# Two chunks of rows gathered ahead of a branch: a two-layer graph convolution on one core

## The chip, the cores and the metric

One core of a Trainium2 chip runs the whole program in one launch. The metric is device time in microseconds of one execution; lower is better. The engines are PE (matrix products and transposes), PEld (PE's weight loads), DVE (vector), ACT (scalar functions), POOL (which here issues the gathers) and SP (which only issues transfers). Each engine works through its own instructions in the order in which the program emits them, and waits where an input or a buffer isn't ready.

## The reference

The graph has 6250 nodes with 128 features and 106250 edges, sorted by their target `dst`. Each edge has 64 attributes and a weight. Two transformer convolutions with 2 heads of 64 follow each other, with a batch normalisation and a ReLU between them; the result is added to x and normalised by rows:

```python
rel_t = last_update[src] - t                       # last_update is node_vec, t is edge_weight
edge_attr = concatenate([cos(rel_t[:, None] * time_w + time_b), msg], -1)    # 32 + 64 columns
# _transformer_conv(h, ...):
q, k, v = h @ Wq + bq, h @ Wk + bk, h @ Wv + bv    # in 2 heads
e = edge_attr @ We
alpha = einsum('ehc,ehc->eh', q[dst], k[src] + e) / sqrt(C)
a = softmax of alpha over the edges of one dst
out = segment_sum((v[src] + e) * a, dst) + h @ Ws + bs
# whole:
h = relu(batch_norm(conv1(x)));   return layernorm(x + conv2(h))
```

So an edge needs the row of features of its source node and, in the first convolution, that node's time.

## The kernel before, in words

**Preparation.** `tile_gnn_resnorm` loads the edge lists (`srows`, `drows`, `erows`: 104 rows of 1024 edges), x and the first convolution's weights. The loads are issued by SP and ACT; every transfer that these two issue uses one of eight semaphores in turn, so an issue waits until the one eight transfers earlier has landed. `columns` turns an edge list so that an edge stands on its partition: `srcs`, `dsts`, `ew`. `load_features` brings x into SBUF in four blocks (`cuts`), in the room that later holds h (`fhT`), with a free column ahead of each row; `pass_features` copies the nodes' times into that column, block by block, and stores rows of 129 numbers to DRAM as `xv_d`. In between, DVE works out the chunks' first nodes (`nbs`) and checks that the edge list has the shape that the fast path needs (`edge`, `worst`, `oki`). Then come `matrices` (products of the weights), `codes`, and `tables` for the first 512 nodes (`tab_d`, `skip_d`).

**The branch.** If the check holds, `ordered` runs; otherwise `general`, which isn't run here.

**`ordered`.** First `turn_features` turns x by 128x128 transposes on PE into `xT`, four to a bank, copied out by DVE and ACT in turn. Then `conv(0)` and `conv(1)` go over 104 chunks of 1024 edges (8 tiles of 128). Per chunk: `fetch` has SP load the attributes, the table and more into the chunk's buffers (`s.f`: the edge's terms `s.e` and its rows `s.x`); `gather` has POOL issue 8 indirect transfers, one for each 128 edges, which bring the source rows from `xv_d` (in `conv(0)`) or from h (in `conv(1)`); `encode` works out the cosine's angles on DVE from the times in column 0 of the rows, and `sine` finishes them on ACT; `turn_rows` and `turn_terms` transpose rows and terms on PE; `score`, `lowest`, `weigh`, `turn_weights`, `gather_sums`, `divide`, `finish_turn` and `product` make the softmax and the sums.

**The order.** It is written out by hand: in round k PE scores chunk k, sums chunk k-1 and turns the rows of chunk k+1, DVE makes the angles of chunk k+2 (later k+3), and POOL gathers chunk k+4 (AHEAD, `lead`). In `conv(0)` rounds -4 to -1 fill the pipeline. From round -1 on the gathers of a chunk are tied one by one to PE's steps of the round (`bring` with `behind`), so that they keep PE's pace. `pull(extra, n)` slips in the work of `rest()`: `targets` (which of a chunk's sums goes to which node) and `tables` for the further blocks of nodes, one product per pull, two pulls in rounds 0 to 3 and one later.

The buffers `ff` come from a pool of 7 in `conv(0)` and of 6 in `conv(1)`.

## Time and profile before

| | |
|---|---|
| median of 3 runs | 2173.48 us (2171.8 to 2174.38) |
| profiled execution, its own time | 2172.61 us |
| its span in the profile | 2170.8 us |
| mean granted clock of PE | 0.878 |
| busy: PE, PEld, DVE, ACT, POOL | 76%, 45%, 51%, 45%, 73% |
| first and last gather of `conv(0)` | 32.77 us, 1070.43 us |
| first gather of `conv(1)` | 1104.59 us |

How to read the rows: in the order of time a row gives start and length in us, engine, line of the kernel, operation, output<-inputs, the number of instructions, and in brackets the idle time ahead and what ended it. SPq and ACTq are the issues of transfers on SP and ACT. In a row of waits stand the sum in us, how often, and the longest. In a row by line stand the count, the shortest, median and longest in ns, and the first and last start in us. In a table of stretches stand each engine's busy us with its count, the granted clock of PE, the share of the transfer engines and GB/s. Releasers are inferred, and where the one named had long been done it was another.

### The profile page before, as it was taken

Reading aid. Unit: us, or ns where it says so; the run is one execution under the profiler, and the core shown is the slowest. Engines: PE = TensorE matmul, PEld = TensorE weight load, DVE = VectorE, ACT = ScalarE, POOL = GpSimd, SP = SyncE. Lnnn points to the kernel's source line nnn. Section 1 sums busy time; section 2 is a strip of 40 time slices with the busy share of each in tenths; the row PEclk is TensorE's granted clock in tenths of the full one; section 3 lists DMA queues with packets and bytes.
Section 4 is the critical chain, followed back from the end, with each engine's and each line's share of the span. In section 5 each row is a group of like instructions: output and inputs, shape, how many; then the busy total and the mean of one; then the engine's idle time right before and its main releaser. Section 6 shows DMA issues by size and latency. Waiting matters only on the chain.

```text
span 2170.8 us, 46552 instructions
## 1 busy us (share of the span) xinstructions
PE 1644.0 (76%) x13253; PEld 975.1 (45%) x13253; DVE 1109.6 (51%) x3706; ACT 970.0 (45%) x1830; POOL 1577.5 (73%) x1684
## 2 busy tenths in 40 slices
PE   4877787867877778787768778777777877777776
PEld 3545454544545445554535434443344434433333
DVE  4866667656666666776747333333333333332233
ACT  1766666655555545566643333333332333232322
POOL 3777777777777777777547777777777777777774
PEclk9899999889999998999988888888888888888888
DMA  7777777777777777777758667676677667667663
GB/s 208 196 223 215 208 227 210 209 198 208 197 208 198 221 214 214 199 216 212 213 161 239 186 180 188 184 198 178 185 192 191 184 188 191 180 189 191 171 162 79
DMA packets 426852, 423.89 MB, mean 195 GB/s; under 512 B 297304, under 2 KB 344258, under 8 KB 423258
## 3 DMA queue, kind: packets, MB, share of 16 engines
q1 hardware_dynamic: 352622, 272.49, 44.0%
q0 software_dynamic: 53184, 109.45, 21.4%
q10 hardware_dynamic: 20780, 38.87, 5.0%
q8 instruction: 109, 1.79, 0.3%
q14 instruction: 157, 1.29, 0.2%
HBM read 274.73 MB, written 142.54 MB: 192 GB/s over the span
## 4 chain that ended last, share of the span: by engine, by line
PE 35%; DMA 35%; DVE 14%; issue 8%; POOL 5%; ACT 2%; SPq 0%; DVEq 0%; ACTq 0%; POOLq 0%
DMA ff<-hn_d,fsrcs 20%; DMA ff<-xv_d,fsrcs 10%; PE fpa L1017 10%; PE fps L970 8%; POOL ff L855 5%; PE fpx L927 5%; PE fpg L632 4%; DVE farg L899 3%; PE fpe L939 2%; PE fpa L1048 2%; DVE fa L1029 1%; PE fppt L994 1%; DVE fangles L897 1%; DVE fangles L896 1%; DVE farg L894 1%
## 5 line engine op out<-in xcount | busy, mean ns | idle before, releaser
L855 POOL DMA_INDIRECT ff<-xv_d,fsrcs x831 | 785.6, 945 | 282.4 <-issue 113.1
L855 POOL DMA_INDIRECT ff<-hn_d,fsrcs x775 | 733.5, 947 | 236.3 <-issue 99.7
L927 PE MATMUL fpx<-fident,ff 128*128 128x128 f32 x1664 | 330.3, 310 | 234.2 <-DMA ff<-hn_d,fsrcs 223.3
L1017 PE MATMUL fpa<-ff,fpt 128*32 128x256 f32 (+1 forms) x4128 | 406.4, 447 | 0.0
L931 ACT COPY fft<-fpx 128x512 f32<-128x512 f32 x402 | 233.2, 580 | 360.0 <-PE fpx L927 357.1
L927 PEld LDWEIGHTS fpx<-fident,ff 128*128 128x128 f32 x1664 | 227.1, 155 | 295.3 <-DMA ff<-hn_d,fsrcs 247.2
L995 ACT COPY fpt<-fppt 128x384 f32<-128x384 f32 x208 | 99.8, 480 | 486.0 <-PE fppt L994 435.6
L970 PE MATMUL fps<-fft,ftab 128*32 128x384 f32 (+1 forms) x1774 | 262.0, 521 | 47.2 <-ACT fs L985 40.5
L1017 PEld LDWEIGHTS fpa<-ff,fpt 128*32 128x32 f32 (+1 forms) x4128 | 141.0, 127 | 263.7 <-issue 186.7
L1048 PE MATMUL fpa<-fsel,fa 128*128 128x128 f32 x404 | 87.9, 302 | 172.8 <-DVE fsel L1033 172.7
L1098 DVE TENSOR_SCALAR fout<-fres,fmean,fvar 64x128 f32<-64x128 f32 x104 | 36.8, 355 | 348.4 <-ACT fvar L1096 342.2
L978 DVE TENSOR_REDUCE flow<-fps 128x1 f32<-128x384 f32 x207 | 114.8, 555 | 83.6 <-PE fps L970 81.9
L939 PE MATMUL fpe<-fident,ff 128*112 128x128 f32 x832 | 145.4, 305 | 2.1 <-ACT ff L906 2.1
L940 ACT COPY fet<-fpe 112x512 f32<-112x512 f32 x207 | 123.1, 595 | 50.4 <-DMA et_d<-fet 34.5
L892 DVE TENSOR_TENSOR frel<-ff,few 128x8 f32<-128x8 f32 x104 | 18.1, 174 | 245.6 <-DMA ff<-xv_d,fsrcs 245.0
L970 PE MATMUL fps<-fet,ftab 112*32 112x384 f32 (+2 forms) x960 | 141.9, 459 | 0.0
L899 DVE SCALAR_TENSOR_TENSOR farg<-fangles,farg 128x256 f32<-128x256 f32 x312 | 132.3, 424 | 10.7
L1048 PEld LDWEIGHTS fpa<-fsel,fa 128*128 128x128 f32 x404 | 48.5, 148 | 193.4 <-DVE fsel L1033 193.3
L970 PEld LDWEIGHTS fps<-fft,ftab 128*32 128x32 f32 x1774 | 85.2, 118 | 108.4 <-ACT fs L985 52.7
L994 PE MATMUL fppt<-fident,fs 128*128 128x128 f32 x626 | 111.5, 288 | 18.2 <-DVE fbits L845 11.2
L985 ACT ACTIVATE fs<-fps,fm 128x384 f32<-128x384 f32 x207 | 120.4, 582 | 6.9 <-DVE fm L980 5.9
L970 PE MATMUL fps<-fxT,ftab 112*32 112x384 f32 (+2 forms) x900 | 119.0, 500 | 0.3 <-DMA fxT<-et_d 0.3
(264 smaller groups left out, 2446.1 us busy)
## 6 DMA issues: line engine op xcount, KB each, us to landing
ea_d<-ff SPq DMA_DIRECT2D x104, 448.0 KB
et_d<-fet SPq DMA_DIRECT2D x104, 448.0 KB
ff<-ea_d SPq DMA_DIRECT2D x104, 448.0 KB
fxT<-et_d SPq DMA_DIRECT2D x104, 448.0 KB
tab_d<-fo ACTq DMA_DIRECT2D x26, 1024.0 KB
ftab<-tab_d SPq DMA_DIRECT2D x832, 32.0 KB
ff<-in_edge_attr SPq DMA_DIRECT2D x103, 256.0 KB
ff<-xv_d,fsrcs POOLq DMA_INDIRECT x831
```

The lines of the kernel that those rows point to most:

```text
L855: row = nc.gpsimd.indirect_dma_start(out=f[:, t, :D + 1 - c], out_offset=None, in_=(h_d[:N, :] if k < RAW else hn_d) if c else pl.xv_d, in ...
L899: nc.vector.scalar_tensor_tensor(arg, turn, -part, arg, op0=OP.mult, op1=OP.add)
L927: last = nc.tensor.transpose(px[:, t * P:(t + 1) * P], s.x[:, u * 4 + t, 1 - c:1 - c + D], ident)
L931: nc.scalar.copy(s.ft[:, u * GE:(u + 1) * GE], px)
L939: last = nc.tensor.transpose(pe[:EC, t * P:(t + 1) * P], s.e[:, u * 4 + t], ident)
L940: copy(s.et[:, u * GE:(u + 1) * GE], pe[:EC])
L970: steps.append(nc.tensor.matmul(s.ps[r, to:to + n], s.tab[:kd, r, i], (ets if i else fts)[:kd, at:at + n], start=i == 0, stop=i == 1 and t ...
L978: nc.vector.tensor_reduce(low, s.ps, AX.X, OP.min)
L985: nc.scalar.activation(s.s[:, :s.ps.shape[1]], s.ps, AF.Exp, bias=s.bias, scale=-1.0)
L994: last = nc.tensor.transpose(pp[:, t * P:(t + 1) * P], s.s[:, t * P:(t + 1) * P], ident)
L1017: steps.append(nc.tensor.matmul(s.pa[g * GH:(g + of) * GH].rearrange("p (a d) -> p a d", a=2), s.pt[:, (g * n + t) * GH:(g * n + t + of) * ...
L1048: step = nc.tensor.transpose(s.po[:, i], s.a[:, r], s.sel[:, 0])
```

## The change

1. **Rows of two chunks ahead of the branch** (EARLY = 2). As soon as `srcs` is there, POOL issues 16 gathers from x itself, into columns 1 to 128 of the first two chunks' rows. The buffers are no longer pool tiles: `got.ring` holds 7 slots (RING) for both convolutions and is made with the program's lasting buffers; `split_rows` hands out a slot. `gather` returns at once for these two chunks, and in `conv(0)` chunks below 7 are no longer tied to PE's steps.
2. **Their times by 0/1 products.** `pick_times` brings the nodes' times as a 49x128 table (`hours`, two more loads on SP). For each 512 edges a product of a 0/1 row with the upper part of the source's number spreads it over 49 partitions, DVE compares it with the lane, four products with `hours` pick the row of 128 times, and four DVE instructions weigh it with the comparison of the lower part and sum it into column 0. They use two banks of their own (`ftm`).
3. **x is turned in the preparation.** `turn_features` becomes a generator with one bank (`fxp`); ACT alone copies. It, `pick_times`, `codes`, `matrices` and `pass_features` are advanced step by step, in an order written out between the steps of the check.
4. **Loads.** `tail` goes behind the weights on ACT; the first 512 rows of x (`x0`) and the edge weights (`erows`) go from ACT to SP, behind x and ahead of the stores to `xv_d`.
5. `matrices` gets twelve pieces of three banks instead of two banks in turn. `targets` takes two pulls instead of one. `columns(drows)` and `columns(erows)` come later. In `conv(1)` there are 7 buffers `ff` instead of 6, `fout` has 4 instead of 6, and `fhn` alternates with `fhr`. `general` takes its room from the ring.

The core of the diff:

```diff
+RING = 7
+EARLY = 2
 def turn_features(nc, pl, bank, N):
-    nc.vector.memset(xT[:, N:], 0.0)
     for b0 in range(0, NF, 4):
-        px = mp.tile([P, 4, P], F32, name="fpx")
+        px = bank().rearrange("p (i n) -> p i n", n=P)
         for i in range(n):
             nc.tensor.transpose(px[:, i], pl.rows[:, b0 + i, 1:], pl.ident)
-        eng = nc.scalar.copy if b0 // 4 % 2 else nc.vector.tensor_copy
-        eng(lanes[:, b0:b0 + n], px[:, :n])
+        nc.scalar.copy(lanes[:, b0:b0 + n], px[:, :n])
+        yield
+def pick_times(nc, pl, pool, bank, srows, node_vec):
+    hi_i = pool.tile([EARLY, CE], I32, name="fhi")
+    nc.vector.tensor_scalar(hi_i, srows[:EARLY], 7, None, op0=OP.arith_shift_right)
...
+    yield
+    for k in range(EARLY):
+        times = split_rows(pl, k)[2]
+        for u in range(T // 4):
+            pb = bank()
+            nc.tensor.matmul(pb[:NA], one[:, k], hi[:, u * GE:(u + 1) * GE], start=True, stop=True)
+            oh = pool.tile([NA, GE], F32, name="foh", bufs=2)
+            nc.vector.tensor_scalar(oh, pb[:NA], lane[:NA], None, op0=OP.is_equal)
+            yield
+            pc = bank().rearrange("p (i n) -> p i n", n=P)
+            for i in range(4):
+                nc.tensor.matmul(pc[:, i], oh[:, i * P:(i + 1) * P], pl.hours, start=True, stop=True)
+            for i in range(4):
+                nc.vector.scalar_tensor_tensor(junk, pl.place_of, lo[:, t, k:k + 1], pc[:, i], op0=OP.is_equal,
+                                               op1=OP.mult, accum_out=times[:, t, 0:1])
+            yield
-            s.f = load.tile([P, T * FW], F32, name="ff")
+            s.f, s.e, s.x = split_rows(pl, k + c * NC)
         def gather(k, rows, behind=None):
             f = ch[k].x
+            if c == 0 and k < EARLY:
+                return
-                        gather(j, rows, behind)
+                        gather(j, rows, behind if c or j >= RING else None)
-        with tc.tile_pool(name="ftp", bufs=3, space=bass.MemoryType.PSUM) as mp, tc.manual_schedule():
-            turn_features(nc, pl, mp, N)
         columns(srows, srcs)
+        for k in range(EARLY):
+            to = split_rows(got, k)[2]
+            for t in range(T):
+                nc.gpsimd.indirect_dma_start(out=to[:, t, 1:], out_offset=None, in_=x,
+                                             in_offset=bass.IndirectOffsetOnAxis(ap=srcs[:, t, k:k + 1], axis=0))
         passed = pass_features(nc, got, made, N)
+        step(hours)
+        step(code)
         picked = pl.tile([NC, 2 * NQ], F32, name="picked")
...
+        step(passed)
+        step(code)
+        step(turned, 2)
         starts = pl.tile([1, NC + 1, NQ], F32, name="starts")
...
+        step(hours)
+        step(passed)
+        step(turned)
+        step(mats, 2)
         edge = pl.tile([1, 11], F32, name="edge")
...
+        step(passed)
+        step(hours)
+        step(turned, 2)
+        step(hours)
         ends = pl.tile([1, 2, NQ], F32, name="ends")
...
+        step(mats)
+        for _ in passed:
+            pass
+        step(turned)
         down = pl.tile([NC, CE], F32, name="down")
...
+        step(mats, 2)
+        pb = small[0][0:1, 0:1]
...
+        for _ in mats:
             pass
         xT0 = pl.tile([P, GE], F32, name="fxT0")
...
+        step(turned)
+        columns(drows, dsts)
+        table = tables(nc, got, 0, xT0, 0, mw, wide)
+        step(table, 4)
+        step(turned)
+        step(hours)
+        columns(erows, ew)
+        step(table)
+        step(hours)
+        step(turned)
+        for _ in hours:
+            step(turned)
+        for _ in turned:
+            pass
```

More of the change, by code (lines that the diff above doesn't have):

```diff
@@ L72, in general @@
 def general(ctx: ExitStack, tc: tile.TileContext, x, src, dst, edge_attr_64, edge_weight, node_vec,
-            time_w, time_b, conv1, conv2, bn_g, bn_b, out):
+            time_w, time_b, conv1, conv2, bn_g, bn_b, out, room, columns):
     nc = tc.nc
@@ L131, in general @@
     nc.sync.dma_start(ew, edge_weight.rearrange("(p j) -> p j", j=EC))
-    xall = const.tile([P, NB, D], F32, name="xall")
+    xall, skip = (room[:, i * NB * D:(i + 1) * NB * D].rearrange("p (b d) -> p b d", d=D) for i in range(2))
     if NR:
@@ L168, in general @@
     step = RW * GT * (-(-64 // GT))
-    zeros = op.tile([P, step], F32, name="zeros")
+    zeros = columns[:, :step]
     nc.gpsimd.memset(zeros, 0.0)
@@ L687, in ordered @@
     et_d = dram.tile([NC, EC, CE], F32, name="et_d")
-    xT = pl.xT = const.tile([P, NP], F32, name="fxT")
+    xT = pl.xT
     def bounds(j):
@@ L877, in hide @@
             for b0 in hidden[:n]:
-                step = put_rows(hn_d, b0, *turned_rows(b0, small.tile([P, GE // P, P], F32, name="fhn", bufs=4)))
+                rows = small.tile([P, GE // P, P], F32, name="fhn", bufs=2) if b0 % 2 else None
+                step = put_rows(hn_d, b0, *turned_rows(b0, rows))
             del hidden[:n]
@@ L1350, in rest @@
             others = second()
-            targets()
+            yield from targets()
             yield
@@ L1493, in tile_gnn_resnorm @@
                                                              ap=[[1, 1], [QE, NQ - i]]))
[L1494 to L1497 removed]
+        x0 = pl.tile([P, GE // P, D], F32, name="fx0")
+        nc.sync.dma_start(x0, x[:GE, :].rearrange("(b p) d -> p b d", p=P))
+        rows(nc.sync, erows, edge_weight, CE)
         got.wv = [keep.tile([P, D], F32, name=f"fwv{c}") for c in (0, 1)]
@@ L1538, in columns, with step @@
                 nc.vector.tensor_copy(to[:, t0:t0 + 4], pt)
+        def step(gen, n=1):
+            for _ in range(n):
+                next(gen, None)
         columns(srows, srcs)
-        passed = pass_features(nc, got, made, N)
+        for k in range(EARLY):
[3 more added lines that the diff above has]
+                                             in_offset=bass.IndirectOffsetOnAxis(ap=srcs[:, t, k:k + 1], axis=0))
+        passed = pass_features(nc, got, made, N)
+        hours = pick_times(nc, got, pl, aside, srows, node_vec)
+        code = codes(nc, got, keep, mw, bank)
+        turned = turn_features(nc, got, turning, N)
+        mats = matrices(nc, got, 0, keep, bank, pl)
+        step(hours)
+        step(code)
         picked = pl.tile([NC, 2 * NQ], F32, name="picked")
@@ L1611, in tile_gnn_resnorm @@
         nc.vector.tensor_scalar(oki, tot, 0.0, None, op0=OP.is_equal)
-        columns(drows, dsts)
-        for _ in matrices(nc, got, 0, keep, bank, pl):
+        for _ in mats:
             pass
-        codes(nc, got, keep, mw, bank)
         pt = wide()
@@ L1621, in tile_gnn_resnorm @@
         nc.vector.tensor_copy(xT0, pt)
-        for _ in tables(nc, got, 0, xT0, 0, mw, wide):
+        step(turned)
[11 more added lines that the diff above has]
+        for _ in turned:
             pass
-        columns(erows, ew)
         got.tw = broadcast(nc, keep, "ftw", time_w, TD)
```

76 lines of the change are left out of this document (50 added, 26 removed).

## The prediction

> **What bounds the kernel now.** I read the row gathers by their line, then what POOL waited for, the order of time at the start and in the first rounds, and the chain of waits there. The profiled execution took 2172.61 us, its span 2170.8; the median of the runs, 2173.48, lies 0.9 above. The sum is made against 2172.61, then carried over. For this kernel 0.2% (4.3 us) is about what a measurement can tell from no change.
>
> ```profile
> L855 POOL DMA_INDIRECT ff<-xv_d,fsrcs x831: 940/944/1121, 32.8 to 1070.4; - x167
> ```
>
> ```profile
> L855 POOL DMA_INDIRECT ff<-hn_d,fsrcs x775: 940/944/1421, 1177.9 to 2146.4; - x194
> ```
>
> ```profile
> POOL ff L855 <- issue: 99.7, 327, 0.3
> ...
> POOL ff L855 <- DMA ff<-xv_d,fsrcs: 18.3, 60, 0.3
> ```
>
> The last fence is what POOL waited for from 100 to 1050 us, the longest wait last: 0.3 us, never more than the gap between two issues. 831 gathers from 32.8 to 1070.4 are one each 1.25 us, and the 775 of convolution 1 that read hn_d keep the same pace. Convolution 0 is a POOL stream: what starts it earlier, or takes gathers from it, ends it earlier, as long as nobody else stands in its way. Convolution 1 follows that end and keeps its length.
>
> **The start, in order of time.**
>
> ```profile
> 8.96 1.28 DVE L1538 CAST fsrcs<-fpx 128x416 int32<-128x416 f32 x2 [1.05 <-PE fpx L1537]
> ...
> 18.68 0.57 DVE L1575 SCALAR_TENSOR_TENSOR most<-prior,nbf 1x412 f32<-1x412 f32 x1
> 19.18 0.07 DVE L1575 DVE_READ_ACCUMULATOR most<-prior,nbf 1x1 f32 x1
> ...
> 20.00 0.34 ACTq L556 DMA_DIRECT2D fbs<-in_L_gnn_bs  x1
> ...
> 20.38 0.59 ACTq L1606 DMA_DIRECT2D fx<-in_x  x1
> ...
> 20.81 3.47 SPq L533 DMA_DIRECT2D xv_d<-fhT  x3
> ...
> 22.62 1.22 DVE L1598 TENSOR_REDUCE worst<-down 104x1 f32<-104x1024 f32 x1
> 23.42 1.02 ACTq L1484 DMA_DIRECT2D erows<-in_edge_weight  x1
> ...
> 24.47 1.28 ACT L588 ACT_TABLE_LOAD   x1 [24.47 <-DMA xv_d<-fxrest]
> 24.55 0.14 DVE L1611 TENSOR_SCALAR oki<-tot 1x1 int32<-1x1 f32 x1
> ...
> 26.68 0.23 PEld L585 LDWEIGHTS fpt<-fident,fwq 128*128 128x128 f32 x1
> ...
> 30.48 0.50 PEld L600 LDWEIGHTS fpt<-ftr,ftr 64*128 64x128 f32 x2 [0.34 <-DVE fb L606]
> ...
> 32.77 1.11 POOL L855 DMA_INDIRECT ff<-xv_d,fsrcs  x1 [29.35 <-DMA fwv<-in_L_gnn_Wv]
> ...
> 35.56 4.46 PE L632 MATMUL fpx<-fxT,fm 128*128 128x512 f32 x6 [0.78 <-DVE fxT L1621]
> ...
> 42.72 0.38 ACTq L644 DMA_DIRECT2D tab_d<-fo  x1
> ...
> 43.96 0.57 PE L1537 MATMUL fpx<-fident,erows 104*128 104x104 f32 x4 [0.69 <-DVE few L1538]
> ...
> 44.58 0.59 DVE L1538 COPY few<-fpx 128x416 f32<-128x416 f32 x1 [0.67 <-PE fpx L1537]
> 45.37 2.31 PEld L658 LDWEIGHTS fpx<-fident,fhT 128*128 128x128 f32 x12 [1.03 <-issue]
> ...
> 48.52 1.02 ACT L660 COPY fxT<-fpx 128x512 f32<-128x512 f32 x1 [4.63 <-DMA ftab<-tab_d]
> ```
>
> POOL has the source columns at 10.2 us but waits until 32.77 for the rows with times (xv_d), whose last store is issued by 24.28. ACT issues loads until 24.44. The flag for the branch stands at 24.69, DVE ends the preparation at 45.17, and only then x is turned, on DVE and ACT.
>
> **The change, part by part.**
>
> *Sixteen gathers leave the stream.* 16 x 1.25 = 20.0 us, done in POOL's idle time from about 10 to 30 us. Their cover is the wait to 32.77; were it gone they would cost those 20 us again.
>
> *Gate 1, the store of xv_d.* It still holds chunk 2. Two things make it later. Transfers:
>
> ```profile
> 0.00:10.00 10.00, 1.65 (x8) 1.33 (x8) 2.42 (x6) 0.00 (x0) 2.74 (x22) 1.00 0.85 194
> 10.00:20.00 10.00, 2.93 (x16) 1.85 (x16) 4.74 (x28) 0.00 (x0) 0.00 (x0) 1.00 1.07 283
> 20.00:30.00 10.00, 4.41 (x21) 3.65 (x21) 6.76 (x30) 2.04 (x4) 0.00 (x0) 1.00 0.92 342
> 30.00:40.00 10.00, 8.02 (x22) 4.39 (x20) 1.86 (x9) 2.87 (x5) 5.71 (x6) 1.00 0.34 74
> ```
>
> ```profile
> q0 software_dynamic: 406, 0.86, 7.9%
> ```
>
> After the five engines' busy times come the granted clock, the DMA share and GB/s: up to 30 us DMA is full (0.85 to 1.07). The gathers of the first 50 us, 0.86 MB, took 7.9% of 50 us, 4.0 us; sixteen (1.05 MB) take 4.8. So at least 32.8 + 4.8 = 37.6. Order: the copies ahead of the stores now stand on DVE behind steps that wait for PE and ACT; the last comes near 36 (below), and the first gather followed the last store's issue by 8.5 us in a full queue, by some 4 in an emptier one. On SP two loads for the times now stand ahead of x and the four loads from ACT ahead of the stores: ACT took 4.1 to issue those four, and all are over well before 36. I take 40, between 37.6 and 45. Alone it ends convolution 0 by 20.0 - (40 - 32.8) = 12.8 us earlier (8 to 15).
>
> *Gate 2, TensorE's first rounds.* Gathers of chunks 2 to 6 now follow nothing but the store and their slots, all free. From chunk 7 on (RING) each follows a step of PE's round four chunks back, as before. What waits behind such a gather is POOL's whole queue, and DVE's angles for its rows.
>
> ```profile
> 60.98 0.51 ACT L906 ACTIVATE ff<-farg,qpi 128x256 f32<-128x256 f32 x1 [0.75 <-DVE farg L900]
> ...
> 61.49 0.17 DVE L892 TENSOR_TENSOR frel<-ff,few 128x8 f32<-128x8 f32 x1
> ...
> 65.25 0.51 ACT L906 ACTIVATE ff<-farg,qpi 128x256 f32<-128x256 f32 x1 [1.25 <-DVE farg L900]
> ```
>
> ```profile
> 77.07 2.08 PE L632 MATMUL fpg<-fxT,fm 128*128 128x512 f32 x2
> ...
> 89.32 0.28 DVE L1033 TENSOR_SCALAR fsel<-fplace,ftarget 128x128 f32<-128x128 f32 x1
> ...
> 93.91 1.65 PE L1017 MATMUL fpa<-ff,fpt 128*64 128x256 f32 x20
> ```
>
> ```profile
> 103.32 0.94 POOL L855 DMA_INDIRECT ff<-xv_d,fsrcs  x1 [0.30 <-issue]
> ```
>
> The gather at 103.32 is chunk 7's first (32.77 + 56 x 1.25 and small gaps); the step it follows, the sums at 93.91, ended at 95.56. Slack: 7.8 us. With gate 1 at 40 POOL wants that gather at 90. So if the rounds move by S, convolution 0's end moves by S - 7.8, unless gate 1 (-12.8) is later. Later PE keeps its lead: from 100 us on POOL waited for it never longer than an issue's gap.
>
> S hangs on E, when DVE ends the preparation. After it: about 0.9 to branch (PE's gap from 44.53, the end of the times' turn, to its weight load at 45.37), 1.1 for constants and marks, 3.75 for the first angles (61.49 to 65.25, the second chunk's, to its sine), then the sine, which stood at 60.98. In round 0 one table product (2.0 us, 77.07) moves a round on because the targets take two steps. S = E + 5.75 - 60.98 - 2.0 = E - 57.2, and the end moves by E - 65.0.
>
> *E, first half: to the flag.*
>
> ```profile
> 11.81 8.18 DMA fhT<-in_x
> ```
>
> In the chain of waits this is x's last block, landing at 20.0: ACT's issue at 20.00 waited for it. The four loads moved to SP (20.38 to 24.44) free ACT at about 20.4; with the table load its first copy of turned x is at 21.7. The turned x has one bank, so each four transposes (a third of 2.31, 0.8) wait for the copy before (1.02), and PE's order puts the times' products behind them. From 21.7: copy and second transposes 1.9; row product 1.5 (4.46 for three); third transposes and copy 1.9; two weights turned 1.0; four hour products 1.6 (a 128-column product is about a quarter of a 512-column one); two more steps of x 2.8; row product 1.5; comparison 0.6; flags and third weight 1.5: the last time copy at 36. Then 2.4 for the order test (twice 1.2) and 1.9 for a matrix unit and the flag's small operations: 40.3, not 24.7. ACT's release is the weak number: if SP's early transfers hold ACT's last issues, 27; if its loads pass sooner, 17.
>
> *E, second half.* Before, flag to end took 20.5 us. Three weights and two of four matrix units have gone ahead (26.68 to 30.48, 3.8), and the codes (some 0.6, five small operations). Added: three times four products with four weighted sums, two row products with a comparison. A weighted sum of 128 columns is not in the trace: between 0.14 (one column, the flag) and 0.64 (412 columns with its accumulator read); I take 0.35, nearest to the 0.28 of a 128-column comparison plus 0.07. So 3 x (0.8 to 1.6 + 1.4) + 2 x (0.8 to 1.5 + 0.6) = 9.4 to 13.2, of which about half lies beside tables and copies of x: 6.5. E = 40.3 + 20.5 - 4.4 + 6.5 = 62.9; its ends are 57 and 71, from ACT's 17 to 27 and PE's clock:
>
> ```profile
> 50.81 7.07 PE L658 MATMUL fpx<-fident,fhT 128*128 128x128 f32 x36 [2.73 <-DVE ff L848]
> ```
>
> ```profile
> 38.70:45.50 6.80, 4.60 (x16) 1.78 (x16) 3.44 (x4) 1.99 (x3) 4.97 (x7) 1.00 0.49 161
> 45.60:55.70 10.10, 7.37 (x35) 6.74 (x34) 5.02 (x14) 3.30 (x4) 7.66 (x9) 0.50 0.64 158
> 55.80:62.60 6.80, 3.89 (x30) 2.96 (x29) 6.40 (x17) 5.41 (x7) 5.27 (x6) 1.00 0.60 130
> ```
>
> In the second stretch, where x is turned with waits between, the granted clock is 0.50; then it is 1.00. The moved transposes will meet both; I mixed them above.
>
> The Trainium skill ("TensorE: Matmul & The Clock Gate", Part 4: PE-mode transpose) says that transposes don't count as busy for the clock gate, so that full rate doesn't engage for them. By that, the moved transposes would hold the preparation at half rate: the products at their upper ends, E some 2 us later, the sum about 0. The trace disagrees: from 50.81 to 57.88 PE does nothing but transposes, and the clock rises from 0.50 to 1.00 within them.
>
> *The rest.* Turning x leaves the time after the branch (13 copies of 1.02, on DVE and ACT in turn); it stands in E. The table of chunk 0 is stored from 42.72 before and from about 55 now, well ahead of its use near 70. Ring of 7 for 6, other buffers for fhn, 4 for 6 of fout: nothing, covered by POOL's unbroken pace in convolution 1, against which DVE there has room; if the cover fails, each wait longer than that room costs itself.
>
> Sum: -20.0 + 7.2 (gate 1) + 10.7 (what gate 2, 62.9 - 65.0 = -2.1, holds back beyond it) = -2.1: 2170.5 for the profiled execution, 2171.4 for the median.
>
> **Rivals.** *The whole stream moves, or nearly.* E under 57, and from 52.2 on gate 1 alone decides: 2161 to 2165.5. For it: DVE is busy for only 1.86 of the 10 us from 30 to 40, so the added work has room. Against: the order of PE and ACT, which the sum above follows. Halfway, E from 57 to 60.7, the time is 2165.5 to 2169.2.
>
> *Slower.* ACT still issues loads when PE holds x's second block, so PE, and DVE behind it, stand until 27 or later. It decides from E = 69.3 on (2177.8): 2179.5 at E = 71. For it: ACT's issues before already waited for x's blocks (x's last, above); against: the four loads are gone from its queue.
>
> *It doesn't do what it says:* the early gathers run, but the store of xv_d lands past 50. Then POOL reaches chunk 7 at 100, and the end moves by -2.8: within the forecast's own range, 2170.7.
>
> **How the numbers follow.** Within 0.2%, E from 60.7 to 69.3: 0.43, with its own range 2169.2 to 2177.8 (the late store's 0.05 in it). Faster, 0.41: whole stream 0.15, halfway 0.26. Slower 0.16. The range, 2163 to 2179, leaves out 0.1 of the whole-stream case below it and 0.08 of the slower one above.
>
> **What would show it.** Sixteen gathers of x between 10 and 31 us; chunk 2's first gather at 38 to 45; a POOL wait of several us near chunk 7, on the sums of PE (absent if the whole stream moved); the first sine at 66 to 71; the last gather of convolution 0 within a few us of 1070.4, and convolution 1 as long as before. Wrong if ACT's first copy of turned x isn't between 19 and 25, if rounds 0 to 3 take another time, or if convolution 1 changes.

## The result, and the profile after

The changed kernel takes 2186.39 us (median of 6 executions, 2181.81 to 2189.09); the kernel before, run beside it, 2173.30. The ratio is 1.0061 (95% interval 1.0047 to 1.0074): 13 us slower, past the forecast's 2171.4 and past its range. The profiled execution took 2188.76 us, with a span of 2187.0. In twelve of the runs below, called the longer runs (e1 to e4, f1, f2, i1 to i4, k2, k3), every kernel, the one before included (2668 to 2673 us), took some 23% longer, with long waits for nothing that the profile shows, so they are compared only with the kernel before beside them, and their traces are read only up to where those waits begin (between 51 and 62 us) or for what ended a wait.

The gathers after the change, by their lines, and what POOL waited for up to 1100 us (sum, times, longest):

```profile
L1610 POOL DMA_INDIRECT fring<-in_x,fsrcs x16: 940/944/1120, 7.8 to 26.9; - x16
```

```profile
L900 POOL DMA_INDIRECT fring<-xv_d,fsrcs x815: 940/944/1057, 45.3 to 1084.9; - x163
L900 POOL DMA_INDIRECT fring<-hn_d,fsrcs x775: 940/944/1795, 1191.9 to 2161.3; - x194
```

```profile
POOL fring L900 <- PE fpa L1063: 39.1, 60, 21.1
...
POOL fring L900 <- DVE fb L606: 17.4, 1, 17.4
```

The sixteen early gathers ran where the forecast put them. Convolution 0's last gather moved from 1070.4 to 1084.9 all the same (+14.5), and convolution 1's from 2146.4 to 2161.3 (+14.9), so convolution 1 kept its length. The stream, unbroken before, now has two holes: 17.4 us ahead of chunk 2 and 21.1 us on PE's sums. In order of time:

```profile
7.76 1.12 POOL L1610 DMA_INDIRECT fring<-in_x,fsrcs  x1 [3.61 <-DVE fsrcs L1600]
...
22.46 1.01 ACT L660 COPY fxT<-fxp 128x512 f32<-128x512 f32 x1
...
38.56 0.17 DVE L532 COPY fhT<-fnv 128x12 f32<-128x12 f32 x1
...
43.56 0.14 DVE L1696 TENSOR_SCALAR oki<-tot 1x1 int32<-1x1 f32 x1
...
45.29 0.94 POOL L900 DMA_INDIRECT fring<-xv_d,fsrcs  x1 [17.42 <-DVE fb L606]
...
73.46 0.08 DVE L706 DVE_READ_ACCUMULATOR fjunk<-fplace,flof,ftm 128x1 f32 x1
...
75.29 0.20 DVE L1153 COPY fangles<-ftw 128x32 f32<-128x32 f32 x1 [1.13 <-ACT fxT L665]
...
80.19 1.28 ACT L952 ACT_TABLE_LOAD   x1 [4.94 <-DVE farg L946]
81.49 0.51 ACT L952 ACTIVATE fring<-farg,qpi 128x256 f32<-128x256 f32 x1
...
98.48 1.52 PE L1016 MATMUL fps<-fft,ftab 128*32 128x384 f32 x8
...
114.33 1.65 PE L1063 MATMUL fpa<-fring,fpt 128*64 128x256 f32 x20
...
116.28 0.94 POOL L900 DMA_INDIRECT fring<-xv_d,fsrcs  x1 [21.14 <-PE fpa L1063]
```

These answer to the rows of the start and the first rounds before: flag 24.55, end of the preparation 45.2, first sine 60.98, scores of round 1 79.08, sums 93.91, chunk 7's first gather 103.32. The preparation ends 28 us late; from the first sine on the rows of PE are some 20 us late, and POOL stands at chunk 7 until the sums have ended. Behind the tables the preparation runs like this on PE (line 659 turns x, 696 and 702 are the products for the times) and on DVE:

```profile
61.40 1.94 PE L696 MATMUL ftm<-fhif,fone 2*49 2x512 f32 x2
63.26 1.11 PE L659 MATMUL fxp<-fident,fhT 128*128 128x128 f32 x4
64.31 2.07 PE L702 MATMUL ftm<-fhours,foh 49*128 49x128 f32 x8
66.31 1.12 PE L659 MATMUL fxp<-fident,fhT 128*128 128x128 f32 x4
67.36 1.94 PE L696 MATMUL ftm<-fhif,fone 2*49 2x512 f32 x2
```

```profile
63.37 0.74 DVE L698 TENSOR_SCALAR foh<-ftm,flane 49x512 f32<-49x512 f32 x1 [3.16 <-PE ftm L696]
66.42 0.35 DVE L706 SCALAR_TENSOR_TENSOR fjunk<-fplace,flof,ftm 128x128 f32<-128x128 f32 x1 [2.30 <-PE ftm L702]
```

One such step takes 6.0 us (61.40 to 67.36), and there are two of them. PE has no gap in a step: its two products and two blocks of x follow one another, and from start to start they are 3.9 and 2.1 us, together the step. DVE's comparison and sums and ACT's copies of x run beside these rows, but PE sets the length: DVE waits 3.2 and 2.3 us for its products.

### The profile page after: what moved, and what is told of

Same layout as the page of the kernel before. It is cut to its first block, busy times and chain, and to the rows that moved or that the text cites. A ratio compares the mean times of both kernels' runs of the same rounds, so it can differ in the third digit from the quotient of the medians.

```text
span 2187.0 us, 45360 instructions
## 1 busy us (share of the span) xinstructions
PE 1667.6 (76%) x13293; PEld 981.9 (45%) x13293; DVE 1113.2 (51%) x3740; ACT 979.0 (45%) x1837; POOL 1578.8 (72%) x1686
## 4 chain that ended last, share of the span: by engine, by line
PE 36%; DMA 33%; DVE 13%; issue 8%; POOL 4%; ACT 3%; SPq 1%; DVEq 0%; ACTq 0%; POOLq 0%
DMA fring<-hn_d,fsrcs 18%; PE fpa L1063 9%; DMA fring<-xv_d,fsrcs 8%; PE fps L1016 8%; PE fpx L973 5%; POOL fring L900 4%; PE fpg L634 3%; DMA et_d<-fet 3%; DVE farg L945 3%; PE fpe L985 2%; PE fpa L1094 2%; PE fppt L1040 1%; DVE fa L1075 1%; ACT L1031 1%; DVE farg L939 1%
## 5 line engine op out<-in xcount | busy, mean ns | idle before, releaser
L900 POOL DMA_INDIRECT fring<-xv_d,fsrcs x815 | 770.4, 945 | 287.5 <-issue 108.2
L900 POOL DMA_INDIRECT fring<-hn_d,fsrcs x775 | 734.5, 948 | 236.2 <-issue 106.7
L973 PE MATMUL fpx<-fident,fring 128*128 128x128 f32 x1664 | 326.9, 306 | 232.1 <-DMA fring<-hn_d,fsrcs 208.8
L1063 PE MATMUL fpa<-fring,fpt 128*32 128x256 f32 (+1 forms) x4128 | 407.7, 448 | 0.0
L973 PEld LDWEIGHTS fpx<-fident,fring 128*128 128x128 f32 x1664 | 223.8, 153 | 294.1 <-DMA fring<-hn_d,fsrcs 247.2
L1016 PE MATMUL fps<-fft,ftab 128*32 128x384 f32 (+1 forms) x1774 | 267.3, 526 | 69.5 <-ACT fs L1031 62.7
L1063 PEld LDWEIGHTS fpa<-fring,fpt 128*32 128x32 f32 (+1 forms) x4128 | 141.6, 128 | 267.5 <-issue 175.9
L985 PE MATMUL fpe<-fident,fring 128*112 128x128 f32 x832 | 145.3, 304 | 5.5 <-ACT fring L952 5.5
L938 DVE TENSOR_TENSOR frel<-fring,few 128x8 f32<-128x8 f32 x104 | 18.2, 175 | 216.0 <-DMA fring<-xv_d,fsrcs 215.1
L1094 PEld LDWEIGHTS fpa<-fsel,fa 128*128 128x128 f32 x404 | 48.7, 147 | 159.7 <-DVE fsel L1079 151.1
```

Of the source, the lines that this page charges most:

```text
L900: row = nc.gpsimd.indirect_dma_start(out=f[:, t, :D + 1 - c], out_offset=None, in_=(h_d[:N, :] if k < RAW else hn_d) if c else pl.xv_d, in ...
L973: last = nc.tensor.transpose(px[:, t * P:(t + 1) * P], s.x[:, u * 4 + t, 1 - c:1 - c + D], ident)
L985: last = nc.tensor.transpose(pe[:EC, t * P:(t + 1) * P], s.e[:, u * 4 + t], ident)
L1016: steps.append(nc.tensor.matmul(s.ps[r, to:to + n], s.tab[:kd, r, i], (ets if i else fts)[:kd, at:at + n], start=i == 0, stop=i == 1 and t ...
L1063: steps.append(nc.tensor.matmul(s.pa[g * GH:(g + of) * GH].rearrange("p (a d) -> p a d", a=2), s.pt[:, (g * n + t) * GH:(g * n + t + of) * ...
L1094: step = nc.tensor.transpose(s.po[:, i], s.a[:, r], s.sel[:, 0])
```

## The experiments

Theory A: the end follows PE's first rounds, which follow the preparation's end, and that is late because one chain of PE, DVE and ACT grew. Rival B: the early gathers, and those of chunks 2 to 6 that no longer keep PE's pace, crowd the transfers. Rival C: the late store of `xv_d` holds the stream.

| kernel | median us | ratio (95%) | flag ends | preparation ends | first sine | sums begin | chunk 7's first gather | last gather of conv 0 |
|---|---|---|---|---|---|---|---|---|
| before | 2173.3 | | 24.7 | 45.2 | 60.98 | 93.91 | 103.32 | 1070.4 |
| changed | 2186.4 | 1.0061 (1.0047 to 1.0074) | 43.7 | 73.5 | 81.49 | 114.33 | 116.28 | 1084.9 |
| g1: changed, again | 2186.5 | 1.0067 (1.0047 to 1.0086) | 44.5 | 71.7 | 79.50 | 110.72 | 112.7 | 1080.2 |
| h1: no products, DVE held | 2183.9 | 1.0051 (1.0034 to 1.0067) | 49.1 | 64.2 | 79.56 | 112.41 | 114.37 | 1082.5 |
| h2: x turned after | 2175.9 | 1.0017 (1.0002 to 1.0033) | 34.3 | 61.4 | 71.30 | 103.88 | 105.83 | 1073.5 |
| h3: neither, DVE held | 2178.9 | 1.0015 (0.9994 to 1.0036) | 42.9 | 58.1 | 73.03 | 106.92 | 108.9 | 1079.0 |
| k1: products over full rows | 2182.6 | 1.0025 (1.0013 to 1.0038) | 42.0 | 66.9 | 74.12 | 106.86 | 108.82 | 1079.4 |
| h4: one chunk early | 2168.1 | 0.9971 (0.9959 to 0.9982) | 32.3 | 47.7 | 62.80 | 96.74 | 98.70 | 1066.5 |

The preparation ends where DVE ends it; in h1 ACT goes on copying x until 73.6. In each changed kernel of the table chunk 7's first gather stands 1.9 to 2.0 us behind the start of the sums, and from it to convolution 0's last gather it is 967 to 971 us everywhere, before included. That is theory A's second half, seven times. The traces give one execution of each kernel, the times all of them. The ratios are against the kernel before on the same chip (for k1 it took 2177.2).

**The changed kernel again (g1).**

> The changed kernel itself, unedited, on the chip on which the experiments run, where the kernel before took 2671 us instead of 2173 in the four and two runs made so far: there the SyncE queue has stretches in which every instruction takes about 0.7 us, which neither first trace shows. It gives the changed kernel's time under these conditions. All theories: if the delay at the start carries over one to one, 2684 to 2690 against 2671 (ratio 1.005 to 1.007); if slow issue hides it, within 4 us of 2671.

The delay is the same. But the two profiled executions of one kernel differ by 3.6 us at the sums; in this one the two steps behind the tables met full clock for longer (below).

**x turned behind the branch (h2).** In `ordered`, `turn_features` gets back its own three banks and copies on DVE and ACT in turn:

```diff
-        turned = turn_features(nc, got, turning, N)
+        turned = iter(())
...
+        with tc.tile_pool(name="ftp", bufs=3, space=bass.MemoryType.PSUM) as mp, tc.manual_schedule():
+            for _ in turn_features(nc, pl, lambda: mp.tile([P, GE], F32, name="fpx"), N):
+                pass
```

> As the changed kernel, but x is turned behind the branch again, with three banks and copies on DVE and ACT in turn; early gathers and products stay. Theory A: the preparation ends some 8 us earlier, but the turning comes back behind it (15.8 us from the end of the preparation to the first sine before, 7.9 after the change): first sine 77 to 83, time 2182 to 2189. If turning x in the preparation is by itself what costs: first sine below 76, time below 2181. Rival B: 2184 to 2189. Rival C: chunk 2 starts earlier, and the time follows it.

```profile
34.16 0.14 DVE L1697 TENSOR_SCALAR oki<-tot 1x1 int32<-1x1 f32 x1
...
61.34 0.08 DVE L706 DVE_READ_ACCUMULATOR fjunk<-fplace,flof,ftm 128x1 f32 x1
...
71.30 0.51 ACT L952 ACTIVATE fring<-farg,qpi 128x256 f32<-128x256 f32 x1
...
103.88 1.65 PE L1063 MATMUL fpa<-fring,fpt 128*64 128x256 f32 x20
...
105.83 0.95 POOL L900 DMA_INDIRECT fring<-xv_d,fsrcs  x1 [18.30 <-PE fpa L1063]
```

The number for theory A missed; the case set beside it holds: turning x in the preparation costs by itself. The preparation ends 12.1 us earlier (g1: 10.3), and only 1.9 us come back behind it (from its end to the first sine 9.9 against 8.0): there the turning has three banks, two engines and the first angles beside it. Most of the gain, 9.4 us, lies ahead of the flag (34.3 instead of 43.7); from the flag to the end it is 27.1 us instead of 29.8. C falls too: chunk 2 started at 37.5 instead of 45.3, and POOL still stood 18.3 us at chunk 7. What releases chunk 2 also differs. In the changed kernel, g1, h1, h3 and k1 its first gather comes 1.6 us behind the flag's end, so it waits for the branch; here, with the flag early, it comes 3.2 us behind, and the trace names a store of `xv_d`.

**No products (h1), neither (h3), and what spoilt them.** `hours = iter(())`, and the column is cleared on DVE:

```diff
-        hours = pick_times(nc, got, pl, aside, srows, node_vec)
+        for k in range(EARLY):
+            nc.vector.memset(split_rows(got, k)[2][:, :, 0:1], 0.0)
+        hours = iter(())
```

> As the changed kernel, but the products that pick the times of chunks 0 and 1 are left out (that column of their rows is 0, so their time angles are not the real ones); early gathers and the turning of x stay in the preparation. Theory A (the first rounds of TensorE start late because the preparation's chain of PE, DVE and ACT has become longer, and from chunk 7 on the gathers follow those rounds): the product steps, 6 us each behind the tables with a copy of x between them that stays, go; first sine from 81.5 to about 72, chunk 7's first gather from 116.3 to about 107, time about 2177 (2174 to 2181). Rival B (the early gathers and the unpaced gathers of chunks 2 to 6 crowd the DMA queues and make rounds 0 to 3 late): time 2184 to 2189. Rival C (the late store of xv_d alone holds the stream): the time moves only as chunk 2's first gather moves.

> Both edits together: no products (the times of chunks 0 and 1 are 0), x turned behind the branch; what is left of the change is the sixteen early gathers, the ring of seven and the reordered loads. Theory A: preparation ends at 45 to 48, first sine 60 to 64, chunk 7's first gather 95 to 99 against 103.3 before and 116.3 after: 4 to 8 us below the kernel before (2165 to 2170). Rival B: 2181 to 2188. Rival C: time follows chunk 2's first gather; at 44, 6 us over the 37.6 of the forecast, 2163 to 2168, with no wait near chunk 7.

Both missed, through the edit itself. DVE's first rows in h3:

```profile
23.08 0.07 DVE L1615 MEMSET fring<- 128x8 f32 x1 [14.48 <-DMA fring<-in_x,fsrcs]
28.56 0.07 DVE L1615 MEMSET fring<- 128x8 f32 x1 [5.41 <-DMA fring<-in_x,fsrcs]
```

The clearing of column 0 waits for the gathers into columns 1 to 128 of the same rows, and DVE with the whole preparation behind it stands for 20 us. With DVE held alike, h1 and h3 still differ by the turning of x: the flag by 6.1 us and the first sine by 6.5. With the clearing on POOL ahead of the gathers (i2, k3) DVE is free:

> No products (column cleared by POOL ahead of the gathers) and x turned behind the branch; what is left of the change is the sixteen early gathers, the ring of seven and the reordered loads. Theory A: first sine 58 to 62, the sums that chunk 7 follows end at 92 to 96, chunk 2 starts at about 37, so the end lies 7 to 10 us under the kernel before: 2163 to 2167. If the early gathers themselves or chunks 2 to 6 without pace hold the rounds back: chunk 7 past 100, 2170 or more.

```profile
32.98 0.14 DVE L1698 TENSOR_SCALAR oki<-tot 1x1 int32<-1x1 f32 x1
...
48.13 0.59 DVE L1601 COPY few<-fpx 128x416 f32<-128x416 f32 x1 [0.25 <-issue]
```

i2's preparation ends at 48.7, 15.6 us behind its flag (33.1); in h1, h3 and h4, also without the products, it is 15.1 to 15.4. In h2, with them, it is 27.1, so the products left behind the flag cost 11.5 us. Ahead of the flag h2 and i2 differ by 1.2 us, less than i2 and k3, the same kernel, differ there (33.1 and 34.8). The times of i2 and k3 are those of longer runs (i2 2672.1, ratio 1.0013, interval 0.9999 to 1.0026; k3 the same ratio), and chunk 7 still waited for the sums. That "neither" would be 6 to 10 us under the kernel before was not measured.

**Products over all rows (k1).** In the steps behind the tables the clock is half while PE is never idle. Clock and busy time of PE in the changed kernel (after the stretch and its length stand PE, PEld, DVE, ACT and POOL, then the granted clock, DMA share, GB/s):

```profile
62.00:65.00 3.00, 3.00 (x9) 1.41 (x8) 0.74 (x1) 0.78 (x2) 2.39 (x3) 0.50 0.54 152
65.00:68.00 3.00, 3.00 (x12) 2.04 (x12) 1.16 (x8) 0.96 (x2) 2.09 (x4) 0.50 0.21 45
68.00:71.00 3.00, 3.00 (x9) 1.44 (x8) 0.74 (x1) 1.10 (x2) 2.39 (x3) 0.50 0.28 61
```

These products work on 2 and on 49 of the 128 rows. The edit fills the rest with zeros, and the spreading product's columns too (49 to 128):

```diff
-    hi = pool.tile([EARLY, CE], F32, name="fhif")
-    nc.vector.tensor_copy(hi, hi_i)
+    hi = pool.tile([P, CE], F32, name="fhif")
+    nc.vector.memset(hi, 0.0)
+    nc.vector.tensor_copy(hi[:EARLY], hi_i)
...
-            nc.tensor.matmul(pb[:NA], one[:, k], hi[:, u * GE:(u + 1) * GE], start=True, stop=True)
+            nc.tensor.matmul(pb, one[:, k], hi[:, u * GE:(u + 1) * GE], start=True, stop=True)
```

> As the changed kernel, but the two kinds of products that pick the times contract over 128 rows instead of 2 and 49 (the rest of the rows is zero), so the result and the count and length of the products stay. Theory H (the clock counts how much of the array works, not whether TensorE is busy): the granted clock stays 1.00 or returns to it within the steps behind the tables, which take 3.6 us each instead of 6; first sine 76 to 78, chunk 7's first gather 109 to 112, time 2177 to 2182. Rival (the clock follows the share of time TensorE is busy, or chance): 0.50 through those steps, first sine 79 to 82, time 2183 to 2189.

```profile
59.34 1.02 PE L697 MATMUL ftm<-fhif,fone 128*128 128x512 f32 x2
60.20 0.60 PE L659 MATMUL fxp<-fident,fhT 128*128 128x128 f32 x4
61.21 1.16 PE L703 MATMUL ftm<-fhours,foh 128*128 128x128 f32 x8 [0.41 <-DVE foh L699]
62.20 0.60 PE L659 MATMUL fxp<-fident,fhT 128*128 128x128 f32 x4
62.64 1.02 PE L697 MATMUL ftm<-fhif,fone 128*128 128x512 f32 x2
```

```profile
59.00:62.00 3.00, 2.59 (x15) 1.59 (x14) 0.75 (x1) 1.72 (x2) 2.39 (x3) 1.00 0.87 282
62.00:65.00 3.00, 2.75 (x18) 1.75 (x17) 1.91 (x9) 1.42 (x2) 2.09 (x4) 1.00 0.28 69
```

The same step takes 3.3 us (59.34 to 62.64) instead of 6.0, at full clock, though PE is busy for less of the time. The clock is 1.00 from 52.7 to 69.7 us here, and 0.50 just ahead of that and behind it; in the changed kernel it is 0.50 from 60.4 to 87.7. The preparation ends 4.9 to 6.7 us earlier, and the ratio falls to 1.0025, outside both intervals of the changed kernel: theory H. By the time alone it is 3.8 us (2186.4 to 2182.6), since the kernel before took 2177.2 on that chip, and 2182.6 is 0.6 above what was expected. In g1, with few rows, the clock was full up to 66 and fell to 0.50 within the products. So one trace with filled rows stands against two with few. The Trainium skill ("TensorE: Matmul & The Clock Gate", Part 1: The HAM clock gate, What's actually happening) gives full rate after one busy window of about 3.4 us; by that the 9 us from 62 to 71, in which PE was busy without a gap, should have had it. The trace disagrees, as long as few-row products are taken as busy.

**No pace (e4 and i4).** `behind if c or j >= 2 * RING else None` in `bring`.

> As the changed kernel, but the gathers of chunks 7 to 13 of convolution 0 do not follow TensorE's steps any more (chunks 2 to 6 did not already); only the ring's slots hold them. Theory A: chunk 7's first row then waits for its slot, read last by the sums of round 0 (106.8 to 108.3) instead of the sums of chunk 1 at 114.3 to 116.0: it starts at about 108.5, the end of convolution 0 moves by about -8, time 2177 to 2180. If the slot's last reader is the sums of chunk 1 as well (they read the last tile of the chunk before), nothing moves: 2184 to 2189. Rival B (unpaced gathers do the harm): more unpaced gathers, rounds later, 2188 to 2195. Rival C: no change.

> As the changed kernel, but the gathers of chunks 7 to 13 of convolution 0 do not follow TensorE's steps any more; only the ring's slots hold them. Theory A: chunk 7's first row waits for its slot, whose rows 0 to 6 are read last by the sums of chunk 0 (end at about 105 to 108), so it starts 6 to 9 us earlier (105 to 109 against 113 to 116), and the time falls by as much: 2175 to 2181. If the slot is held whole until the sums of chunk 1: 2182 to 2189, no change. If unpaced gathers do harm to the rounds: over 2189.

The time itself (e4 1.0168, i4 1.0196, both longer runs) says little, but the wait at chunk 7 is the same without the tie (e4):

```profile
150.99 1.65 PE L1063 MATMUL fpa<-fring,fpt 128*64 128x256 f32 x20
```

```profile
152.46 0.95 POOL L900 DMA_INDIRECT fring<-xv_d,fsrcs  x1 [54.50 <-PE fpa L1063]
```

So the slot of the ring, which these sums read last, holds the gather just as the tie does. Unpaced gathers did not help in these runs; by their ratios both are 1.0 to 1.8% above the other variants run beside them.

**One chunk early, times by gathers (h4).** The full computation: `EARLY = 1`, no products, x turned behind the branch, and in POOL's idle time eight more gathers of one number each:

```diff
+            for t in range(T):
+                nc.gpsimd.indirect_dma_start(out=to[:, t, 0:1], out_offset=None, in_=node_vec.rearrange("(n o) -> n o", o=1),
+                                             in_offset=bass.IndirectOffsetOnAxis(ap=srcs[:, t, k:k + 1], axis=0))
```

> The full computation in another way: only chunk 0 early; its times come by eight more gathers of one number per row from the time vector, in POOL's idle time, instead of by products; x is turned behind the branch. Theory A: sixteen gathers from 8 to 28, chunk 1 starts at about 35 behind the store of xv_d, POOL wants chunk 7's first gather at 95; first sine 57 to 62, the sums that gather follows end at 92 to 97: convolution 0 ends 5 to 9 us earlier than before, 2164 to 2169. Rival B: slower than before, as the changed kernel. Rival C: time follows chunk 1's first gather: at 35, 2165 to 2167, at 45 no gain.

```profile
29.52 0.95 POOL L1610 DMA_INDIRECT fring<-in_node_vec,fsrcs  x1 [0.30 <-issue]
36.13 0.94 POOL L900 DMA_INDIRECT fring<-xv_d,fsrcs  x1 [5.67 <-DVE fb L606]
...
98.70 0.94 POOL L900 DMA_INDIRECT fring<-xv_d,fsrcs  x1 [2.17 <-PE fpa L1063]
```

The time came as expected: 2168.06 us, ratio 0.9971, 0.3% under the kernel before. The first sine at 62.8 and the sums, which end at 98.4, came a little later than expected. The preparation ends at 47.7, and POOL waits 2.2 us instead of 21.1 at chunk 7. Early gathers and chunks without pace are in it too, so B falls.

**The longer runs.** Kernels of the table and near ones were measured here too, most with times expected as in the shorter runs; the ratios are to the kernel before beside them. As h1, h2 and h3:

> As the changed kernel, but the products that pick the times of chunks 0 and 1 are left out (that column of their rows is set to 0, so their time angles are not the real ones); the early gathers and the turning of x stay in the preparation. Theory A (the rounds of TensorE start late because the preparation's chain PE, DVE, ACT has become longer, and from chunk 7 on the gathers follow those rounds): the two product steps behind the tables (about 6 us each, with a copy of x between that stays, 2.3 each) and those ahead of the flag go; first sine from 81.5 to about 72, chunk 7's first gather from 116.3 to about 107, time about 2177 (2174 to 2181). Rival B (the 16 early gathers and the unpaced gathers of chunks 2 to 6 crowd the DMA queues and make rounds 0 to 3 late): first sine earlier, but chunk 7 and the time as the changed kernel, 2184 to 2189. Rival C (the late store of xv_d alone holds the stream): the time moves only as the first gather of chunk 2 moves.

> As the changed kernel, but x is turned behind the branch again, with three banks and copies on DVE and ACT in turn, as in the kernel before; early gathers and products stay. Theory A: the preparation ends some 8 us earlier (about 65 instead of 73.5), but the turning comes back behind it (from the end of the preparation to the first sine 15.8 us before, 7.9 after the change): first sine 77 to 83, time 2182 to 2189, about the changed kernel's. If turning x in the preparation is by itself what costs, the first sine comes below 76 and the time below 2181. Rival B: no change. Rival C: chunk 2 starts earlier, and the time follows it.

> Both edits together: no products for the times of chunks 0 and 1 (the column is 0) and x turned behind the branch; what is left of the change is the sixteen early gathers, the ring of seven and the reordered loads. Theory A: the preparation ends as in the kernel before (45 to 48), first sine 60 to 64, chunk 7's first gather 95 to 99 against 103.3 before and 116.3 after, time 2164 to 2170, under the kernel before. Rival B: chunk 7 past 110 and time 2181 to 2188 although the first sine is early. Rival C: time follows chunk 2's first gather: at 37 to 40 that is 2174 to 2180.

> As the changed kernel, but without the products for the times of chunks 0 and 1 (the column is 0, so their time angles are not the real ones) and with x turned behind the branch by DVE and ACT in turn; what is left of the change is the sixteen early gathers, the ring of seven and the reordered loads. Theory A (the end follows the first rounds of TensorE, which follow the end of the preparation): preparation ends at 45 to 48, first sine 60 to 64, chunk 7's first gather 95 to 99 against 103.3 before and 116.3 after; 4 to 8 us below the kernel before, 17 to 21 below the changed one. Rival B (early and unpaced gathers crowd the queues): rounds late, time within 5 us of the changed kernel. Rival C (the late store of xv_d): the time follows chunk 2's first gather, 7 us over 37.6 costs 7.

e1 2691.6 us, ratio 1.0064; e2 2683.4, 1.0041; e3 2682.4, 1.0035; f1 2679.3, 1.0030. All missed their times. POOL's waits for PE over the whole run (in e1 119.9 us for the sums, 106.4 for the turned rows, 99.4 for the scores) suggest that PE's rounds, not POOL, set the pace there; this was not tested. As h4 and k1:

> The full computation in another way: only chunk 0 early; its times come by eight more gathers of one number per row from the time vector, in POOL's idle time, instead of by products; x is turned behind the branch as before. Theory A: sixteen gathers from 7.8 to 28, then POOL waits for xv_d until 33 to 40 and chunk 1 starts there; preparation and first sine as in the kernel before or a little earlier (57 to 62); POOL wants chunk 7's first gather at 93 to 100 and the sums it follows end at 92 to 97, so convolution 0 ends 3 to 10 us earlier than before: 2163 to 2171. Rival B: as the changed kernel, slower than before. Rival C: the time follows the store of xv_d: chunk 1 at 45 or later would cost what was won (2173 or more).

> As the changed kernel, but the two kinds of products that pick the times contract over 128 rows instead of 2 and 49 (the rest of the rows is zero), so the result and the count and length of the products stay. Theory H (the clock counts how much of the array's rows works, not whether TensorE is busy): the granted clock stays 1.00 or returns to it within the steps behind the tables, which take 3.6 us each instead of 6; first sine 76 to 78, chunk 7's first gather 109 to 112, time 2177 to 2182. Rival (the clock follows the share of time TensorE is busy, or chance): 0.50 through those steps as before, first sine 79 to 82, time 2183 to 2189.

f2 2683.2, ratio 1.0050: here that kernel is slower than the one before, not faster. i3 2694.4, 1.0096: its steps behind the tables lie where the long waits begin. With the clearing on POOL, x turned in the preparation (i1, k2) and behind the branch (k3, as i2):

> As the changed kernel without the products for the times of chunks 0 and 1, but the column is set to 0 by POOL ahead of the gathers (their time angles are not the real ones); before, the clearing on DVE waited for the gathers and held DVE from 8.6 to 28.6, which delayed the flag to 48.9. Theory A: flag at about 38 instead of 43.6, behind the tables only the copies of x stay; first sine 68 to 73, chunk 7's first gather 102 to 107, time 2171 to 2177. Theory A' (the products cost nothing beside the one chain of x's turning): first sine 77 to 80, 2180 to 2185.

> As the changed kernel without the products for the times of chunks 0 and 1; the column is set to 0 by POOL ahead of the gathers (their time angles are not the real ones), so DVE doesn't wait for them. Theory A: flag at about 39 instead of 43.6, behind the tables only the copies of x stay; preparation ends at 62 to 67, first sine 69 to 74, chunk 7's first gather 102 to 108, time 2172 to 2178. Theory A' (the products cost nothing beside the one chain of x's turning): first sine 77 to 80, 2180 to 2185.

> No products (column cleared by POOL ahead of the gathers) and x turned behind the branch; what is left of the change is the sixteen early gathers, the ring of seven and the reordered loads. Theory A: preparation ends at about 50, first sine 59 to 63, the sums that chunk 7 follows end at 92 to 97, chunk 2 starts at about 37.5, so the end lies 6 to 10 us under the kernel before: 2163 to 2168. If the early gathers themselves or chunks 2 to 6 without pace hold the rounds back: chunk 7 past 100, 2170 or more.

i1 2680.9, ratio 1.0044; k2 2680.5, 1.0043; k3 2672.8, 1.0013. i1 and k2 have the flag at 39.6 and 43.3 us (43.7 in the changed kernel) and reach the last table product at 56.1 and 59.0; then the long waits begin. So what x's turning costs without the products, with DVE free, is known only up to the flag: against i2's and k3's flags (33.1 and 34.8) 4.8 to 10.2 us.

## Why the prediction was wrong

- *Bound, second gate and rule: right.* Convolution 0 follows two gates, the second at chunk 7 on PE's sums, with 7.8 us of slack, and convolution 1 keeps its length. The sums moved by S = 20.4, less 7.8 is 12.6, and chunk 7's first gather moved by 13.0. Up to the last gather another 1.5 was lost, 0.75 of it in one hole, ahead of the gather at 678.4 us.
- *Gate 1: close, but by another mechanism.* Last time copy 38.6 (forecast 36), chunk 2 at 45.3 (37.6 to 45). It was not the store that held it: the gather came 1.6 us behind the flag's end and so waited for the branch, as in four other traces; in h2, where the store did hold it, it came at 37.5. That the forecast nearly met 45.3 is luck. It decided nothing.
- *E, first half: nearly right.* ACT's first copy of x at 22.5 (21.7), flag at 43.7 (40.3): +3.4. Turning x is 9.4 us of that flag (34.3 in h2), and the forecast had priced this part.
- *E, second half: the step that failed.* "About half lies beside tables and copies of x: 6.5" for products, and nothing for the blocks of x still to be turned. Flag to end took 29.8 us, not 22.6. What is left without products is about as forecast: 15.6 (i2; forecast 20.5 - 4.4 = 16.1). The products cost 11.5 (h2 against i2), within the forecast's own 9.4 to 13.2 but with hardly any of it hidden: in h2 their rows on PE behind the flag add up to 8.3 us, and PE's waits for DVE between them to 3.0. The blocks of x add 2.7 (29.8 against h2's 27.1; only 0.1 in g1, where the clock fell later). The order of PE put a block of x between each pair of products, and PE had no gap in which the one could hide the other. E = 73.5, not 62.9 and past the upper end of 71.
- *PE's clock* was named as an uncertainty of E, and mixed. It was half for both steps that set the end (0.50 for 27 us without a break). With the rows filled (k1) flag to end is 24.9 us, so of the 7.2 us missed there some 5.0 go with the half clock. The sentence of the Trainium skill that the forecast weighed ("TensorE: Matmul & The Clock Gate", Part 4: PE-mode transpose: transposes don't count for the clock) was not the cause: k1 has the same transposes and full clock in both steps; the few-row products made the difference.
- *S from E.* E to the first sine took 8.0 us instead of 5.75: DVE waited 1.1 for ACT's last copy of x, and the sine's table load (1.28), which before ran at 58.95 beside DVE's last steps for the angles, now waited until they were done (80.19). The table product that left round 0 gave 1.1 of its 2.0 (first sine +20.5, scores of round 1 +19.4), and round 1 lost 1.0 again (sums +20.4). Together 4.1.
- *Rivals.* The slower side had the right rule (decides from E = 69.3) but the wrong mechanism, ACT still issuing loads: its issues ended at 21. The measured E in the forecast's own rule gives 73.5 - 65.0 = +8.5, 2182; the missing 4.1 of S bring 2186. That this meets the median is partly luck: the profiled execution lies 16.2 above the one before, 13.0 of it at chunk 7, 1.5 up to the last gather, 0.4 in convolution 1 and 1.3 behind its last gather.

Of S = 20.4 against the forecast 5.7, E is 10.6 (3.4 up to the flag, 7.2 behind it) and the path from E to the sums 4.1.

## What to carry to other kernels

Idle shares of engines are no room for a chain: a step that hops between PE, DVE and ACT costs nearly its full length unless an engine's gap falls at just the place where the other work stands, so write out the order of the engine in the middle before halving a price, and price the step at the clock that the stretch will have. When work is pulled ahead of a stream, ask which later gate the stream then meets, and spend nothing on the way that delays it: h4 pulled half as many gathers ahead, added eight, left the turning of x behind the branch, and won. Small products on few rows were dear here, where the clock stayed low with them; filling the rows with zeros is worth a try where other work shares the stretch.

## What the runs showed of the hardware

- A product over 2 or 49 of 128 rows doesn't hold TensorE's clock up: 0.50 for 27 us with PE busy without a gap from 62 to 71, and 1.00 from 53 to 70 once the rows were filled (one trace). The 512-column products' own length hardly depends on the rows (a pair takes 1.05 us in g1 and 1.02 in k1 at full clock). Whether rows or columns count was not told apart.
- Transposes raise it: in h2 the turning of x begins at 61.6, and the clock went from 0.50 to 1.00 at 66.2; before, it began at 50.8, and the clock rose at 55.8.
- A gather of 128 rows keeps POOL busy for 0.94 us, and one follows each 1.25 us; in h4 that is so for rows of 516 bytes and for single numbers of 4 bytes alike.
- Slow issue. In the longer runs PE, DVE, ACT and SP had stretches with long waits for nothing that the profile shows. Issues on SP and the turning of x behind the branch in f1, and below them the same issues in h3, the same kernel:

```profile
65.94 9.80 SPq L874 DMA_DIRECT2D ftab<-tab_d  x4
```

```profile
83.85 1.11 PE L659 MATMUL fpx<-fident,fhT 128*128 128x128 f32 x4 [9.38 <-issue]
```

```profile
64.57 1.94 SPq L874 DMA_DIRECT2D ftab<-tab_d  x4
```

Four issues take 9.80 us instead of 1.94, and PE stands 9.4 us between two blocks. POOL had such waits too, but of 3.2 us at most in the traces read (i1). What brings it about stays open.
